# Edge attention in a graph transformer: exponentials kept in PSUM, gathers of 128 rows, and a first stage with its transfers rearranged

## The chip, the cores and the metric

The kernel runs on one core of a Trainium2 chip. A core has five engines with instruction queues of their own: TensorE (PE, matrix products and transposes), the vector engine (DVE), ScalarE (ACT), GpSimd (POOL) and SyncE (SP), which here only issues transfers. Engines wait for one another by semaphores. Transfers run on 16 DMA engines that the core's queues share. Data lie in SBUF, matrix products land in PSUM, and tables between stages are in DRAM. The metric is the device time of one execution in microseconds (us), given as a median of several runs; lower is better.

## The reference

The input is a graph with 3125 nodes of 256 features and 100,000 edges, sorted by their target node, with 64 features on each edge. Two layers follow one another. Layer 0 adds an edge attention and a mixer to the node features, then a mixture of experts; layer 1 adds a graph convolution, a linear-attention mixer and a feed-forward part on selected rows. The changed lines belong to layer 0. Its edge attention is:

```python
Q = (h @ Wq).reshape(n, H, HD)          # h = layernorm(x), H = 8 heads, HD = 32
K = (h @ Wk).reshape(n, H, HD)
V = (h @ Wv).reshape(n, H, HD)
score = jnp.einsum('ehd,ehd->eh', Q[dst], K[src]) / np.sqrt(HD)
score = score + jax.nn.relu(efeat @ W1 + b1) @ W2 + b2
m = jax.ops.segment_max(score, dst, num_segments=n)
ex = jnp.exp(score - m[dst])
denom = jax.ops.segment_sum(ex, dst, num_segments=n)
alpha = ex / denom[dst]
out = jax.ops.segment_sum(alpha[:, :, None] * V[src], dst, num_segments=n)
return out.reshape(n, D) @ Wo + bo
```

`x = x + attention(layernorm(x)) + mixer(layernorm(x))` follows, where the mixer ends with a bias `b2`; so the two constant rows `bo` and `b2` can be added to `x` early.

## The kernel before, in words

**Node rows.** The 3125 nodes are held as 125 partitions by 25 tiles. `X` is a view of them over three big SBUF tiles, `KV0` to `KV2`, which later serve as buffers of gathered rows.

**First stage (up to about 350 us).** Weights and small rows are loaded; a row that is copied to all partitions comes by `load_row` (L176). `b2` and `bo` are summed (L313), and their column form `bcol` too (L314). A loop of five steps normalises the rows (L316 to L325); GpSimd adds the normalised row and `b2` to `X` (L323, L324). A Python generator, `tables()`, builds index tables from the sorted edges: it loads the source and target nodes, the target of the next edge (`nxt`, L338 to L342), and near its end runs four indirect loads on GpSimd (`we`, L495), whose results TensorE transposes and the vector engine copies (L502). The projection loop over 25 tiles (L546 to L566) takes three steps of that generator per tile, projects keys and values into a DRAM table `kv_tab`, and queries, split in three bfloat16 parts, into `q_tab`; the split subtracts on GpSimd (L565). Then come the zero fills of the DRAM tables `o_tab`, `og_tab`, `y_tab` (L575, issued by ScalarE) and `moe_in` (L577, L579, issued by GpSimd), though the scheduler that orders each engine's instructions may place them earlier, as they depend on nothing but their zero tile. A loop over the 25 tiles computes keys and values of the mixer (L611 to L625), with vector engine, ScalarE and TensorE in turn, and a last one adds the mixer to `X` (L675 to L687). `move` (L162) is the helper that stores and loads tables in pieces.

**Edge stage (about 396 to 1710 us).** The edges are cut into 40 groups of 20 tiles of 125 edges; the 20 tiles are four runs of five. One pass of the loop (L875 to L988) handles a group. Here an order is written out by hand for TensorE (`pe`), and the vector engine's order is that of the program with the scheduler's moves. The steps, with the lines that the change or the prediction touches:

- SP loads the edge features two groups ahead (`load_features`, L763), and query rows and target indices of the group.
- GpSimd gathers one row of `kv_tab` (key and value, 512 numbers) for each edge: 20 indirect loads of 125 rows (L901), into one of ten `KV` buffers per run. Ten buffers of five tiles let 50 gathers run ahead.
- TensorE copies each edge's query from the window of target nodes (L911); the vector engine multiplies it with the gathered key, reading the query in PSUM (L914), and sums over the head (L924). In between, TensorE and ScalarE compute the next group's hidden edge features (L783, L785).
- The maximum over the group is found (L929 to L942) and subtracted (L944).
- ScalarE takes the exponential of each of the four runs and writes it next to the value columns of the `KV` buffer (L948); the vector engine multiplies the values with it (L950); TensorE sums the products by target node with a one-hot matrix (L953), for two runs in turn.
- The sums are laid into a window, divided and stored (L715, L719, L971 onward). The next group's one-hot matrix (L697) may be written only when L953 has read the present one.

Lines that say how the gathered rows, the exponentials and the sums are joined:

```python
ex = kvs[r][:, :, 2 * D:2 * D + H]
nc.scalar.activation(ex, sc[:, r * KB:(r + 1) * KB, :], AF.Exp)
v = kvs[r][:, :, D:2 * D].rearrange("p g (h d) -> p g h d", d=HD)
nc.vector.tensor_tensor(v, v, ex[:, :, :, None].to_broadcast([P, KB, H, HD]), ALU.mult)
```

Later stages (about 1710 us to the end) build the adjacency matrix (L1295), run the experts and layer 1; of the change only `load_row` reaches them.

Of the kernel before, what the change touches and what calls it, by code (L numbers as in the profile page):

```python
# [9 lines left out]
F32 = mybir.dt.float32  # L10
BF16 = mybir.dt.bfloat16
I32 = mybir.dt.int32
# [65 lines left out]
def kernel(ctx: ExitStack, tc: tile.TileContext, a, out):  # L78
# [38 lines left out]
    def row(t, shape):  # L117
        return t[:, None, :].to_broadcast(shape)
# [54 lines left out]
        nc.sync.dma_start(t, src.rearrange("(c p) n -> p c n", p=128))  # L173
        return t

    def load_row(pool, src, name, parts=P):  # L176
        n = 1
        for s in src.shape:
            n *= s
        t = pool.tile([parts, n], F32, name=name)  # L180
        nc.sync.dma_start(t, rows_of(src, parts))
        return t

    def rstd(o, var, scale=1.0):

# [86 lines left out]
    lgx = keep.tile([P, T, NE], F32, name="lgx")  # L272

    x1 = ctx.enter_context(tc.tile_pool(name="x1", bufs=1))
    KV = [x1.tile([P, KB, 2 * D + H + 1], F32, name=f"KV{i}") for i in range(3)]
    X = Rows(KV)
    with_edges = ctx.enter_context(ExitStack())
    edges = with_edges.enter_context(tc.tile_pool(name="edges", bufs=1))
    srcs = edges.tile([P, NG * GT], I32, name="srcs")
    dl = edges.tile([P, NG * GT], F32, name="dl")  # L280
    first = edges.tile([128, NG * NR], F32, name="first")
    runpos = edges.tile([128, NG], F32, name="runpos")
# [13 lines left out]
    with tc.tile_pool(name="a1", bufs=1) as a1, tc.tile_pool(name="a2", bufs=2) as a2, \  # L296
# [13 lines left out]
        bcol = a1.tile([128, 2, 2], F32, name="bcol")  # L310
        for i, n in enumerate(("L0_mix_b2", "L0_gnn_bo")):
            nc.scalar.dma_start(bcol[:, i, :], a[n].rearrange("(c p) -> p c", p=128))
        nc.vector.tensor_add(b2, b2, bo)  # L313
        nc.vector.tensor_add(bcol[:, 0, :], bcol[:, 0, :], bcol[:, 1, :])  # L314
        std = a1.tile([P, T], F32, name="std")
        for g in range(0, T, 5):  # L316
            xn = a2.tile([P, 5, D], F32, name="xn")
            mv, rs = layernorm(a2, xn, X[:, g:g + 5, :], "ln0")
            nc.scalar.activation(mean0[:, g:g + 5], mv[:, :, 0], AF.Copy)
            nc.vector.reciprocal(std[:, g:g + 5], rs)  # L320
            nc.scalar.activation(std[:, g:g + 5], std[:, g:g + 5], AF.Copy, bias=1.0)
            for i in range(5):
                nc.gpsimd.tensor_add(X[:, g + i, :], X[:, g + i, :], xn[:, i, :])  # L323
                nc.gpsimd.tensor_add(X[:, g + i, :], X[:, g + i, :], b2)  # L324
            transpose_tokens(pa, xT[:, :, g:g + 5, :], xn)  # L325
        def tables():

            with tc.tile_pool(name="c0", bufs=1) as c0:
# [6 lines left out]
                with tc.tile_pool(name="c1", bufs=1) as c1:  # L335
                    nxt = c1.tile([RP, 2 * RUN], I32, name="nxt")
                    nc.vector.memset(nxt, N)
                    yield  # L338
                    after = a["dst"][1:]
                    n = (RP - 1) * 2 * RUN  # L340
                    nc.scalar.dma_start(nxt[:RP - 1, :], after[:n].rearrange(flat, p=RP - 1))
                    nc.scalar.dma_start(nxt[RP - 1:, :2 * RUN - 1], after[n:].rearrange(flat, p=1))  # L342
                    nc.vector.tensor_tensor(nxt, nxt, dr, ALU.is_lt)
                    yield
# [201 lines left out]
        for t in range(T):  # L546
            for _ in range(3):
                next(edge_tables, None)
            ps = pa.tile([128, 512], F32, name="mm", bufs=2)
            mm(ps[:P], [(xT[:, k, t, :], wkv[:, k, :]) for k in range(2)])  # L550
            kvt = a2.tile([P, 2 * D], F32, name="kvt", bufs=3)
            evac(kvt, ps[:P])
            move(nc.sync, kv_rows[:, t, :], kvt)

            ps = pa.tile([128, 512], F32, name="mm", bufs=2)
            mm(ps[:P, :DG], [(xT[:, k, t, :], wq[:, k, :]) for k in range(2)])

            nc.vector.scalar_tensor_tensor(lgx[:, t, :], ps[:P, D:DG], std[:, t:t + 1], gb, op0=ALU.mult, op1=ALU.add)
            q = a2.tile([P, D], F32, name="q", bufs=3)
            nc.scalar.activation(q, ps[:P, :D], AF.Copy, scale=1.0 / math.sqrt(HD))  # L560
            q3 = a2.tile([P, 3, D], BF16, name="q3", bufs=3)
            for i in range(3):
                nc.scalar.activation(q3[:, i, :], q, AF.Copy)
                if i < 2:
                    nc.gpsimd.tensor_sub(q, q, q3[:, i, :])  # L565
            move(nc.sync, q_rows[:, t, :], q3.rearrange("p i d -> p (i d)"))  # L566
        for _ in edge_tables:
            pass


        zero = a3.tile([128, D + 2], F32, name="zero")
        nc.gpsimd.memset(zero[:, :D + 1], 0.0)
        nc.gpsimd.memset(zero[:, D + 1:], SKIP)
        for tab, w in ((o_tab, D), (og_tab, NE + 1), (y_tab, D)):
            move(nc.scalar, tab[:N].rearrange("(p t) c -> p t c", t=T), row(zero[:P, :w], [P, T, w]))  # L575
        whole = NE * CAP // 128 * 128
        nc.gpsimd.dma_start(moe_in[:whole].rearrange("(p k) d -> p k d", p=128),  # L577
                            row(zero, [128, whole // 128, D + 2]))
# [143 lines left out]
    with tc.tile_pool(name="l1", bufs=1) as l1, tc.tile_pool(name="l2", bufs=2) as l2, \  # L722
# [12 lines left out]
        KV = KV + [l1.tile([P, KB, 2 * D + H + 1], F32, name=f"KV{i}") for i in range(3, NKV)]  # L735
# [24 lines left out]
        efTs, hids, scts, biases = {}, {}, {}, {}  # L760

        def load_features(g):
            nc.sync.dma_start(EF[g % 2][:, :FJ, :].rearrange("p j f -> p (j f)"), efv[:, g, :])  # L763

        def turn_features(g):
            efT = efTs[g] = l2.tile([128, PF, F2], F32, name="efT")
# [108 lines left out]
        for g in range(NG):  # L875
# [17 lines left out]
            for z in range(2):  # L893
                pair = []
                for r in range(2 * z, 2 * z + 2):
                    kv = KV[nkv % NKV]
                    nkv += 1
                    pair.append(kv)
                    for i in range(KB):
                        e = g * GT + r * KB + i  # L900
                        nc.gpsimd.indirect_dma_start(out=kv[:, i, :2 * D], out_offset=None, in_=kv_tab,  # L901
                                                     in_offset=indirect(srcs[:, e:e + 1]))
# [39 lines left out]
            nc.vector.tensor_max(top, old, tps[:, :H])  # L942
            tops.append(top)
            nc.vector.tensor_sub(sc, sc, row(top[:P], [P, GT, H]))  # L944
            for z in range(2):
                for r in range(2 * z, 2 * z + 2):
                    ex = kvs[r][:, :, 2 * D:2 * D + H]
                    nc.scalar.activation(ex, sc[:, r * KB:(r + 1) * KB, :], AF.Exp)  # L948
                    v = kvs[r][:, :, D:2 * D].rearrange("p g (h d) -> p g h d", d=HD)
                    nc.vector.tensor_tensor(v, v, ex[:, :, :, None].to_broadcast([P, KB, H, HD]), ALU.mult)  # L950
                for i in range(KB):
                    for r in range(2 * z, 2 * z + 2):
                        pe(nc.tensor.matmul(seg[r * W:(r + 1) * W, :], oh[:, r * KB + i, :], kvs[r][:, i, D:],  # L953
                                            start=i == 0, stop=i == KB - 1))
# [968 lines left out]
```

## Time and profile before

| | us |
|---|---|
| median of three runs | 2893.51 (2891.22 to 2893.81) |
| profiled execution | 2897.13 |
| its span, first instruction to last | 2895.3 |
| busy in the span: TensorE / vector engine / GpSimd / ScalarE | 2240.8 / 1875.0 / 1364.6 / 934.7 |
| mean granted TensorE clock | 0.897 |
| edge stage, first product L914 | from 396.1 |
| last multiplication L950 begins | 1700.2 |
| bytes moved by DMA | 340 MB, 118 GB/s in the mean |

The profiled execution is one run taken with the hardware profiler. A line of its page that names a group reads: source line, engine, operation, what is written and read, how often; then busy time, mean duration of one in ns; then the idle time of that engine just before these instructions, and what ended most of it ("releaser"). A line of waits reads: engine, what waited and its line, for which engine and line; total us, times, longest. A line of the timeline reads: start, duration, engine, line, operation, what is written and read, how many in a row; in brackets the idle time before and its releaser. A line of one group's durations gives the shortest, the median and the longest in ns, then the start of the first and of the last.

### The profile page before, as it was taken

The numbers are of one execution on the slowest core, as the hardware profiler recorded it, in microseconds if no ns is written. First come the engines' busy times: TensorE is split into PE (matmuls) and PEld (weight loads), VectorE is DVE, ScalarE is ACT, GpSimd is POOL, SyncE is SP. The second block draws the span as 40 slices with busy tenths as digits, with TensorE's granted clock in tenths as the row PEclk, the third lists the DMA queues.
The fourth block names the chain that finished last, engine by engine and source line by source line (L and its number), as shares of the span: only waits on it lengthen the run. The fifth ranks groups of instructions, "written<-read, shape, count | busy, mean of one in ns | idle before, by whom it ended". The sixth has DMA issues, their size and how long they took to land. (4 is left out here: it accounts for less than half of the span.)

```text
span 2895.3 us, 40359 instructions
## 1 busy us (share of the span) xinstructions
PE 2240.8 (77%) x14013; PEld 1404.5 (49%) x14013; DVE 1875.0 (65%) x4137; ACT 934.7 (32%) x1838; POOL 1364.6 (47%) x1172
## 2 busy tenths in 40 slices
PE   2588777777777777787777744799689999978894
PEld 1244434444444444444444323465457775756673
DVE  4748337777777777777777658343478844846446
ACT  0243133333333333333333304212163323243331
POOL 3444368888888887788888712211100002221110
PEclk9788869999998999989999866899899999999997
DMA  7740488888888888888888842233200002000001
GB/s 187 159 126 17 109 192 191 183 193 190 188 193 190 187 195 187 190 188 189 191 194 191 184 111 85 79 98 105 55 2 5 5 1 70 2 1 1 1 19 48
DMA packets 272347, 340.23 MB, mean 118 GB/s; under 512 B 156170, under 2 KB 203437, under 8 KB 271534
## 3 DMA queue, kind: packets, MB, share of 16 engines
q0 software_dynamic: 185600, 219.53, 33.4%
q1 hardware_dynamic: 72794, 101.95, 13.5%
q10 hardware_dynamic: 13732, 16.01, 2.2%
q8 instruction: 114, 1.87, 0.3%
q14 instruction: 107, 0.88, 0.1%
HBM read 294.80 MB, written 43.25 MB: 117 GB/s over the span
## 5 line engine op out<-in xcount | busy, mean ns | idle before, releaser
L901 POOL DMA_INDIRECT KV<-kv_tab,srcs x800 | 1077.4, 1347 | 330.2 <-issue 148.9
L914 DVE TENSOR_TENSOR KV<-KV,qe 125x512 f32<-125x512 f32 (+1 forms) x480 | 266.3, 595 | 154.9 <-PE qe L911 142.9
L953 PE MATMUL seg<-KV,oh 125*32 125x265 f32 x1600 | 267.6, 525 | 126.3 <-DVE KV L950 115.6
L785 ACT ACTIVATE hid<-hidden,b1e 128x910 f32<-128x910 f32 (+1 forms) x240 | 249.5, 1039 | 304.0 <-PE hidden L783 304.0
L911 PE MATMUL qe<-q,ohT 64*125 64x256 bf16 x2400 | 220.2, 280 | 98.5 <-DVE KV L914 95.5
L911 PEld LDWEIGHTS <-ohT 64*125 64x125 bf16 x2400 | 159.7, 134 | 218.3 <-issue 210.8
L783 PE MATMUL hidden<-efT,w1e 64*128 64x455 f32 (+1 forms) x960 | 240.3, 574 | 16.1 <-ACT hid L785 14.7
L953 PEld LDWEIGHTS seg<-KV,oh 125*32 125x32 f32 x1600 | 133.0, 143 | 244.7 <-DVE KV L950 160.8
L924 DVE TENSOR_REDUCE sc<-KV 125x40 f32<-125x1280 f32 x160 | 229.9, 1478 | 0.0
L950 DVE TENSOR_TENSOR KV<-KV 125x1280 f32<-125x1280 f32 x160 | 227.9, 1487 | 1.5 <-ACT KV L948 1.4
L1493 PE MATMUL sum<-adj,f 125*128 125x400 bf16 (+1 forms) x1050 | 197.2, 328 | 0.0
L1295 PE MATMUL build<-oc,op 128*125 128x200 bf16 x1176 | 144.0, 262 | 55.9 <-ACT xn L214 41.4
L192 DVE TENSOR_TENSOR op<-values,ends_of 128x756 bf16<-128x756 bf16 x196 | 108.3, 553 | 93.4 <-PE build L1295 91.5
L1295 PEld LDWEIGHTS <-op 128*125 128x125 bf16 x1176 | 125.8, 144 | 82.3 <-ACT xn L214 41.5
L1493 PEld LDWEIGHTS <-f 125*128 125x128 bf16 x1200 | 115.7, 98 | 102.9 <-issue 31.2
L192 DVE TENSOR_TENSOR oc<-values,ends_of 128x1200 bf16<-128x1200 bf16 x196 | 152.3, 777 | 0.0
L1562 POOL DMA_DIRECT2D ln_cols<-in_L_mix_ln_g_dram x1 | 0.8, 787 | 316.3 <-DVEq L1513 316.3
L1298 ACT ACTIVATE adj<-build 125x400 bf16<-125x400 f32 x171 | 86.0, 504 | 186.0 <-PE build L1295 186.0
L715 ACT ACTIVATE u<-seg 128x265 f32<-128x265 f32 x40 | 15.7, 393 | 332.3 <-PE seg L953 332.3
L1619 PE MATMUL mm<-bt,fw 128*128 128x250 f32 (+1 forms) x416 | 100.8, 405 | 26.4 <-DVE bt L110 23.3
L265 PE MATMUL mm<-bt,w 128*128 128x489 f32 x256 | 110.5, 582 | 5.1 <-ACT bt L112 3.3
L265 PE MATMUL mm<-w,hT 128*128 128x256 f32 (+1 forms) x512 | 112.6, 379 | 0.0
(462 smaller groups left out, 3910.4 us busy)
## 6 DMA issues: line engine op xcount, KB each, us to landing
EF<-in_edge_attr_dram SPq DMA_DIRECT2D x40, 625.0 KB
w<-in_L_ffn_w_dram SPq DMA_DIRECT2D x16, 1024.0 KB
KV<-kv_tab,srcs POOLq DMA_INDIRECT x800
q<-q_tab SPq DMA_DIRECT2D x160, 48.0 KB
dlb<-dl_tab SPq DMA_DIRECT2D x160, 39.1 KB
kv_tab<-kvt SPq DMA_DIRECT2D x25, 224.0 KB
o_tab<-ow SPq DMA_DIRECT2D x40, 128.0 KB
q_tab<-q SPq DMA_DIRECT2D x25, 168.0 KB
```

Of the source, the lines that this page charges most:

```text
L192: nc.vector.tensor_tensor(dst.rearrange("p n (m o) -> p n m o", o=2), values.rearrange("p (u m o) -> p u m o", u=1, o=2).to_broadcast([dst ...
L265: nc.tensor.matmul(o, l, r, start=i == 0, stop=i == len(pairs) - 1)
L783: pe(nc.tensor.matmul(ps[:, s, :n * F2], w1e[f, c * 128:(c + 1) * 128], efTs[g][f, p0:p0 + n, :], start=True, stop=True))
L785: nc.scalar.activation(hids[g][:, c, p0:p0 + n, :].rearrange("h p (f s) -> h s p f", s=2), ps[:, :, :n * F2].rearrange("h s (p f) -> h s p ...
L901: nc.gpsimd.indirect_dma_start(out=kv[:, i, :2 * D], out_offset=None, in_=kv_tab, in_offset=indirect(srcs[:, e:e + 1]))
L911: pe(nc.tensor.matmul(ps[:, i, :], ohT[w, z, (i0 + i) * P:(i0 + i + 1) * P], q3[w, z, k, :], start=k == 0, stop=k == 2))
L914: nc.vector.tensor_mul(kv[:, i0:i0 + nt, :D], kv[:, i0:i0 + nt, :D], ps[:, :nt, :])
L924: nc.vector.tensor_reduce(sc[:, r0:r0 + KB, :], kv[:, :, :D].rearrange("p g (h d) -> p g h d", d=HD), AX.X, ALU.add)
L950: nc.vector.tensor_tensor(v, v, ex[:, :, :, None].to_broadcast([P, KB, H, HD]), ALU.mult)
L953: pe(nc.tensor.matmul(seg[r * W:(r + 1) * W, :], oh[:, r * KB + i, :], kvs[r][:, i, D:], start=i == 0, stop=i == KB - 1))
L1295: pe(nc.tensor.matmul(ps[:, j // CT, :], op[:, j, :P], oc[:, j, :], start=j % CT == 0, stop=j % CT == CT - 1))
L1493: pe(nc.tensor.matmul(sps[c][:, :n], f3[:, t, i, c * 128:(c + 1) * 128], adj[:, t, :n], start=t == 0 and i == 0, stop=t == T - 1 and i == 2))
```

## The change

Four edits come together.

1. **Exponentials.** Per group two exponentials of two runs each replace four of one run. They are written to a PSUM tile that shares the buffer name `score` with the tile of the edge scores. The vector engine's multiplication reads them there, and ScalarE copies them run by run from PSUM to the columns of the `KV` buffer that L953 reads.
2. **Gathers.** The `KV` buffers and the index table have 128 partitions instead of 125; each gather moves 128 rows. The three additional indices are set to zero, and what they bring is not read.
3. **Edge features.** A group's load of 100 partitions is issued as two, of 96 and of 4.
4. **First stage.** `load_row` loads 128 partitions everywhere. The sums with `bo` stand behind the layernorm loop, and `b2` is added to `X` in a loop of its own. The load of `nxt`, 79 partitions, is issued as 64 and 15. The zero tile is tied behind the last query subtraction of the projections, so that the zero fills can't start before; three of the four tables are now filled by SP's queue instead of ScalarE's.

```diff
-    def load_row(pool, src, name, parts=P):
+    def load_row(pool, src, name):
...
-        t = pool.tile([parts, n], F32, name=name)
-        nc.sync.dma_start(t, rows_of(src, parts))
-        return t
+        t = pool.tile([128, n], F32, name=name)
+        nc.sync.dma_start(t, rows_of(src, 128))
+        return t[:P]
...
-    srcs = edges.tile([P, NG * GT], I32, name="srcs")
+    all_srcs = edges.tile([128, NG * GT], I32, name="srcs")
+    nc.gpsimd.memset(all_srcs[96:], 0)
+    srcs = all_srcs[:P]
...
-        nc.vector.tensor_add(b2, b2, bo)
-        nc.vector.tensor_add(bcol[:, 0, :], bcol[:, 0, :], bcol[:, 1, :])
...
-                nc.gpsimd.tensor_add(X[:, g + i, :], X[:, g + i, :], b2)
             transpose_tokens(pa, xT[:, :, g:g + 5, :], xn)
+        nc.vector.tensor_add(bcol[:, 0, :], bcol[:, 0, :], bcol[:, 1, :])
+        nc.vector.tensor_add(b2, b2, bo)
+        for t in range(T):
+            nc.gpsimd.tensor_add(X[:, t, :], X[:, t, :], b2)
...
+                    for p0, p1 in ((0, (RP - 1) // 16 * 16), ((RP - 1) // 16 * 16, RP - 1)):
+                        nc.scalar.dma_start(nxt[p0:p1, :],
+                                            after[p0 * 2 * RUN:p1 * 2 * RUN].rearrange(flat, p=p1 - p0))
                     n = (RP - 1) * 2 * RUN
-                    nc.scalar.dma_start(nxt[:RP - 1, :], after[:n].rearrange(flat, p=RP - 1))
...
-                    nc.gpsimd.tensor_sub(q, q, q3[:, i, :])
+                    rest = nc.gpsimd.tensor_sub(q, q, q3[:, i, :])
...
-        nc.gpsimd.memset(zero[:, :D + 1], 0.0)
-        nc.gpsimd.memset(zero[:, D + 1:], SKIP)
+
+        for x in (nc.gpsimd.memset(zero[:, :D + 1], 0.0), nc.gpsimd.memset(zero[:, D + 1:], SKIP)):
+            tc.add_manual_dep(x.ins, rest.ins.name, NOSYNC, reason="zeros behind the projections")
         for tab, w in ((o_tab, D), (og_tab, NE + 1), (y_tab, D)):
-            move(nc.scalar, tab[:N].rearrange("(p t) c -> p t c", t=T), row(zero[:P, :w], [P, T, w]))
+            move(nc.sync, tab[:N].rearrange("(p t) c -> p t c", t=T), row(zero[:P, :w], [P, T, w]))
...
-            nc.sync.dma_start(EF[g % 2][:, :FJ, :].rearrange("p j f -> p (j f)"), efv[:, g, :])
+            for r in (slice(0, PF // 16 * 16), slice(PF // 16 * 16, PF)):
+                nc.sync.dma_start(EF[g % 2][r, :FJ, :].rearrange("p j f -> p (j f)"), efv[r, g, :])
...
-                        nc.gpsimd.indirect_dma_start(out=kv[:, i, :2 * D], out_offset=None, in_=kv_tab,
-                                                     in_offset=indirect(srcs[:, e:e + 1]))
+                        nc.gpsimd.indirect_dma_start(out=whole[:, i, :2 * D], out_offset=None, in_=kv_tab,
+                                                     in_offset=indirect(all_srcs[:, e:e + 1]))
...
+            exps = pl.tile([128, 3, P], F32, name="score")[:P].rearrange("p a b -> p (a b)")
+            exps = exps[:, :GT * H].rearrange("p (j h) -> p j h", h=H)
             for z in range(2):
+                part = slice(2 * z * KB, 2 * (z + 1) * KB)
+                nc.scalar.activation(exps[:, part, :], sc[:, part, :], AF.Exp)
                 for r in range(2 * z, 2 * z + 2):
-                    ex = kvs[r][:, :, 2 * D:2 * D + H]
-                    nc.scalar.activation(ex, sc[:, r * KB:(r + 1) * KB, :], AF.Exp)
+                    ex = exps[:, r * KB:(r + 1) * KB, :]
                     v = kvs[r][:, :, D:2 * D].rearrange("p g (h d) -> p g h d", d=HD)
                     nc.vector.tensor_tensor(v, v, ex[:, :, :, None].to_broadcast([P, KB, H, HD]), ALU.mult)
+                    nc.scalar.activation(kvs[r][:, :, 2 * D:2 * D + H], ex, AF.Copy)
```

The rest of the diff gives the ten `KV` buffers 128 partitions (`WHOLE`), with `KV` as their first 125.

More of the change, by code (lines that the diff above doesn't have):

```diff
@@ L274 @@
     x1 = ctx.enter_context(tc.tile_pool(name="x1", bufs=1))
-    KV = [x1.tile([P, KB, 2 * D + H + 1], F32, name=f"KV{i}") for i in range(3)]
+    WHOLE = [x1.tile([128, KB, 2 * D + H + 1], F32, name=f"KV{i}") for i in range(3)]
+    KV = [t[:P] for t in WHOLE]
     X = Rows(KV)
@@ L734 @@
             nc.sync.dma_start(b2e[W * c:W * c + H, :], a["L0_gnn_b2"].rearrange("(h o) -> h o", o=1))
-        KV = KV + [l1.tile([P, KB, 2 * D + H + 1], F32, name=f"KV{i}") for i in range(3, NKV)]
+        WHOLE = WHOLE + [l1.tile([128, KB, 2 * D + H + 1], F32, name=f"KV{i}") for i in range(3, NKV)]
+        KV = [t[:P] for t in WHOLE]
         for t in KV:
@@ L895 @@
                 for r in range(2 * z, 2 * z + 2):
-                    kv = KV[nkv % NKV]
+                    kv, whole = KV[nkv % NKV], WHOLE[nkv % NKV]
                     nkv += 1
```

## The prediction

> **What bounds the kernel now.** I read the page's costliest groups first, then the vector engine's waits inside the edge stage (400 to 1710 us), then one group of that stage in order of time, then the stretches of the first stage. The edge stage is 45% of the span and takes two of the parts changed. Its groups on the page:
>
> ```profile
> L901 POOL DMA_INDIRECT KV<-kv_tab,srcs x800 | 1077.4, 1347 | 330.2 <-issue 148.9
> L914 DVE TENSOR_TENSOR KV<-KV,qe 125x512 f32<-125x512 f32 (+1 forms) x480 | 266.3, 595 | 154.9 <-PE qe L911 142.9
> L953 PE MATMUL seg<-KV,oh 125*32 125x265 f32 x1600 | 267.6, 525 | 126.3 <-DVE KV L950 115.6
> L924 DVE TENSOR_REDUCE sc<-KV 125x40 f32<-125x1280 f32 x160 | 229.9, 1478 | 0.0
> L950 DVE TENSOR_TENSOR KV<-KV 125x1280 f32<-125x1280 f32 x160 | 227.9, 1487 | 1.5 <-ACT KV L948 1.4
> ```
>
> GpSimd's gathers (L901) are the largest sum, 1077 us, so GpSimd looks like the bound. The vector engine's waits say otherwise:
>
> ```profile
> DVE KV L914 <- PE qe L911: 139.2, 196, 1.4
> DVE oh L697 <- PE seg L953: 114.8, 38, 4.1
> ...
> DVE KV L914 <- issue: 7.4, 1, 7.4
> DVE KV L914 <- DMA KV<-kv_tab,srcs: 4.6, 6, 1.1
> ```
>
> It waits 139 us for TensorE's query products and 115 us (38 times, 3.0 each) for the segment sums, and 12 us in all for gathers. L950 starts at 416.3 first and 1700.2 last: 39 groups in 1284 less 5, 32.8 us each. GpSimd needs 20 x (1.347 + about 0.3 between two gathers) = 32.9 for the same, so it falls slowly behind: counted in the trace, 39 gathers are issued ahead at the first group and 18 near the end, out of 50 that ten buffers allow. The lead nearly lasts. What sets the pace is the chain vector engine, TensorE, ScalarE within a group. Its softmax part, from the timeline of one group:
>
> ```profile
> 934.12 0.61 ACT L948 ACTIVATE KV<-sc 125x40 f32<-125x40 f32 x4 [0.57 <-DVE sc L944]
> ...
> 934.39 5.70 DVE L950 TENSOR_TENSOR KV<-KV 125x1280 f32<-125x1280 f32 x4
> ...
> 934.99 1.96 POOL L901 DMA_INDIRECT KV<-kv_tab,srcs  x1 [0.30 <-DMA KV<-kv_tab,srcs]
> ...
> 937.25 2.51 POOL L901 DMA_INDIRECT KV<-kv_tab,srcs  x1 [0.31 <-DMA KV<-kv_tab,srcs]
> 937.34 5.31 PE L953 MATMUL seg<-KV,oh 125*32 125x265 f32 x32 [0.31 <-DVE KV L950]
> 940.07 1.18 POOL L901 DMA_INDIRECT KV<-kv_tab,srcs  x1 [0.30 <-DMA KV<-kv_tab,srcs]
> ...
> 943.36 0.83 DVE L697 TENSOR_TENSOR oh<-dl,iota 125x640 f32<-125x640 f32 x1 [3.27 <-PE seg L953]
> ```
>
> The four exponentials run ahead of the four multiplications, which stand back to back (5.70). Then the vector engine waits 3.27 until the sums that follow the last of them are done. Beside L950 a gather takes 1.96 and 2.51 instead of 1.2; L950 itself never takes over 1494 ns.
>
> **Part 1, exponentials by way of PSUM.** Two exponentials of 125x80 replace four of 125x40, and four ScalarE copies of 125x40 bring the result into the columns that the segment sums read. All lie in one PSUM tile. In the built program each copy waits for its run's multiplication, the next multiplication for that copy, the second exponential for the second copy. So the phase is one file: exp, mul, copy, mul, copy, exp, mul, copy, mul, copy. Durations: the multiplication 1.487 (L950; the product L914 reads PSUM and takes 0.68 for 512 columns, L950 1.487 for 1280: the same 1.05 ns per column, so PSUM as an input costs nothing); exp of 125x40 0.226, of 1x8 0.19, hence 125x80 about 0.26; a copy out of PSUM of 125x64 0.22 and of 125x96 0.25 (L808), hence 125x40 about 0.20; each hand-over ScalarE to vector engine and back about 0.03. The phase becomes 4 x 1.487 + (0.20+0.06) + (0.20+0.26+0.09) + (0.20+0.06) = 7.02 against 5.70: +1.32. The first exponential is 0.03 longer. The last run's sums wait for its copy: +0.23. Given back: the first pair's sums now have 3.5 instead of 3.0 us before the last pair's, so less is queued: 0.25. Sum +1.33 per group, x 40 = **+53 us**. Ends: group by group the tail from last multiplication to last sum is 2.48 to 4.09, mean 3.01; if all fall to 2.48, 1.58 - 0.53 = +1.05 (+42); if TensorE, less busy, takes all at the slow end, 1.58 + 1.08 = +2.66 (+106). I take the middle as the tail keeps its nine matmuls (two records each) of some 0.31: in the timeline 19 run from 937.34 to 943.32.
>
> Here a rule of the Trainium skill is weighed ("PSUM — Partial Sum Buffer", section on bank collisions): two engines on one bank and partition quadrant must be kept apart, two readers too. The row is L948's four in 0.61 with 1.4 us of waiting for ScalarE in the whole stage: in SBUF both read freely. By that row the copies would run beside the next multiplication and only 0.03 + 0.23 be added, +10 us over 40 groups. By the rule +53. The waits in the built program follow the rule, so I take it.
>
> **Part 2, gathers of 128 rows; L950 with one SBUF input.** Another rule speaks for the change ("SBUF — State Buffer", "Who interferes with whom"): a vector instruction with two SBUF inputs contends with a GpSimd instruction that reads SBUF, one with a single SBUF input does not. The two stretched gathers above agree: 0.76 + 1.31 = 2.1 us per group. Rows for the size:
>
> ```profile
> L1442 POOL DMA_INDIRECT y_tab<-yr,who x32: 974/982/1071, 1856.5 to 2075.8; - x32
> L1385 POOL DMA_INDIRECT moe_in<-xn,pi x25: 1191/1194/1695, 1784.8 to 1823.6; - x25
> ```
>
> 128 rows are issued in 0.98, 125 rows in 1.19. GpSimd's need falls to 20 x 1.28 + 0.9 (L192, L697 still stretch some) = 26.5 per group. If GpSimd set the pace, 20 x 0.22 + 2.1 = 6.5 x 40 = 260 us could go; by the waits only the 12 us for gathers can: **-12** (0 to -13). 2.4% more rows raise the DMA share from 0.83 to 0.85 in a longer period: nothing, covered by the lead of the gathers; without cover 2.4% of 27 us busy, 0.6 per group.
>
> **Part 3, features.** 96 + 4 rows instead of 100: SP issues one more DMA of 0.33 per group, loaded two groups ahead: 0; SP has no wait on the path there.
>
> **Part 4, first stage.** The zero fills (10.2 MB) move from the first 130 us to behind the projections' last query subtraction (L565), the large one still on GpSimd's queue, the others from ScalarE's to SP's; the bias sums move behind the layernorm; one more GpSimd loop adds b2 (same 25 additions, moved).
>
> ```profile
> DVE bcol L314 <- DMA bcol<-in_L_gnn_bo_dram: 17.5, 1, 17.5
> DVE b L313 <- DMA bo<-in_L_gnn_bo_dram: 11.9, 1, 11.9
> ...
> 100.00:150.00 50.00, 23.48 (x48) 11.23 (x48) 31.98 (x38) 12.34 (x29) 12.08 (x16) 0.69 0.83 177
> 150.00:210.00 60.00, 53.05 (x149) 27.74 (x150) 24.36 (x52) 30.32 (x76) 25.70 (x37) 0.93 0.48 142
> 210.00:275.00 65.00, 56.14 (x199) 30.87 (x198) 59.84 (x108) 21.53 (x46) 34.10 (x27) 0.92 0.08 28
> ```
>
> (columns of the last three: length, busy of TensorE, its loads, vector engine, ScalarE, GpSimd, granted clock, DMA share, GB/s.) L565 runs from 90.8 to 204.2; from 163 on it takes 3.11 per tile, so 25 tiles are worth 78 and 35 are lost to waits while the DMA engines are full. With GpSimd's wait of 16.1 for the bias, at most 35 + 16 = 51 us can go. But at 210 to 275 the vector engine is the bound (59.84 of 65), and that stage's work does not shrink. It also gets work: the table steps that were spread over the projections stand in it, and they wait for four indirect loads on GpSimd's queue (L495), of which the second stands behind the 3.87 MB zero fill. That fill took 31 us in the first stage (2.88 to 33.88); now it shares the engines with 6.25 MB more from SP, and at the 177 to 240 GB/s seen, 10 MB take 42 to 57. With the projections' end near 152 (204 - 51), the second load lands near 195 to 205 and the vector engine stands until then, with the key and value products (L621, L623) queued behind it. Then 60 us of that stage (as now, 213.9 to 273.9) end at 255 to 265 instead of 274: -9 to -19. Some tiles of it can run before the stall: **-18**. Ends: -50 if the second load slips past the fill, +8 if the fills also hold SP's stores of the tables.
>
> **Part 5, rows of 128 partitions in load_row.** One such load (mb) stands 6.9 us on the chain at 2395.5; halved or so: **-2** (0 to -5).
>
> **Sum:** +53 - 12 - 18 - 2 = +21. The profiled execution took 2897.13 (span 2895.3 and 1.8 around it), 3.6 above the median; differences carry over, so 2893.5 + 21 = **2914 us**, and a profile near 2918.
>
> **The rivals.** *First stage wins (faster).* The serial file costs its low end, +42, and the zero fills don't hold the vector engine: -50 - 12 - 4. Net -24: 2869. It turns at one point, whether the second indirect load waits for the 3.87 MB: below zero once the first stage gives more than 39 at +53, or more than 28 at +42. For it: 51 us of waits; against: one queue. *TensorE slows.* Every tail at 4.09: +106 - 12 - 18 - 2 = +74: 2968. For it: TensorE idles some 0.5 us more between pairs, and its clock row varies from 0.69 to 0.93 by stretch; against: in the mean the tail is 3.01. *The file isn't one.* Copies beside multiplications: +10 - 12 - 18 - 2 = -22: 2871; against it the waits in the built program. *It evens out* at 2893: first stage -40 with +53 - 12.
>
> **How the numbers follow.** Likeliest 0.60 (its own range 2898 to 2935), first stage wins 0.18, file isn't one 0.05, evens out 0.07, TensorE slows 0.10. Two per mille, 5.8 us, is about what a measurement can tell from no change. Faster 0.18 + 0.05 = 0.23; same 0.07; slower 0.60 + 0.10 = 0.70. Range: half of the faster cases are cut below 2870, and half of the slow end above 2962.
>
> **What would show it.** Right: the multiplication (L964) stays at 1.49 with gaps of 0.26, 0.55, 0.26 in a group and 7.0 us in all; gathers at 0.98 and none of 2 us beside L964; a period near 34.1; waits of L914 for gathers gone; the vector engine idle for some 35 us for the second indirect load; first product (L924) near 378 instead of 396. Wrong: multiplications back to back, a period under 33.5 or over 35, or a kv stage that ends before 245.

## The result, and the profile after

The changed kernel takes 2932.95 us (median of four, 2928.93 to 2939.47), the kernel before beside it 2893.49: ratio 1.0139, interval 1.0121 to 1.0156. It is slower by 39.5 us; 21 were forecast. Two later comparisons gave 1.0149 (1.0131 to 1.0166) and 1.0139 (1.0108 to 1.0170).

The two profiled executions lie nearer: spans of 2927.1 and 2895.3, 31.8 apart. The execution profiled before was 3.6 above its median, the one after (2928.93) 4.0 below its own; 31.8 + 3.6 + 4.0 = 39.4. By stretches of the span:

| us | before | after | difference |
|---|---|---|---|
| start to first query product | 396.1 | 378.0 | -18.1 |
| first product to end of the last value multiplication | 1305.6 | 1356.9 | +51.3 |
| from there to the end | 1193.6 | 1192.2 | -1.4 |

The groups on the page after, in the form of those shown of before (L924 is now the product, L964 the multiplication, L965 the copy, L968 the sums, L911 the gathers):

```profile
L911 POOL DMA_INDIRECT KV<-kv_tab,srcs x800 | 760.0, 950 | 653.6 <-PE seg L968 398.3
L968 PE MATMUL seg<-KV,oh 125*32 125x265 f32 x1600 | 315.5, 565 | 147.0 <-ACT KV L965 147.0
L924 DVE TENSOR_TENSOR KV<-KV,qe 125x512 f32<-125x512 f32 (+1 forms) x480 | 265.9, 595 | 148.6 <-PE qe L921 148.6
...
L964 DVE TENSOR_TENSOR KV<-KV,score 125x1280 f32<-125x1280 f32 x160 | 238.1, 1488 | 45.8 <-ACT score L960 23.9
...
L965 ACT ACTIVATE KV<-score 125x40 f32<-125x40 f32 x160 | 33.1, 207 | 243.7 <-DVE KV L964 243.7
```

GpSimd's gathers are busy 760 us instead of 1077, and GpSimd now waits 398 us ahead of them for the sums that free its buffers: it is far ahead. The multiplication takes 1488 ns as before, but has 45.8 us of idle time where it had 1.5. The vector engine's waits from 400 to 1750 us:

```profile
DVE KV L924 <- PE qe L921: 142.2, 194, 1.4
DVE oh L705 <- PE seg L968: 126.5, 38, 3.5
...
DVE KV L964 <- ACT score L960: 22.6, 43, 0.5
DVE KV L964 <- ACT KV L965: 21.9, 80, 0.3
```

The two waits that the prediction counted as waits for gathers (7.4 and 4.6) are gone; two for ScalarE have come, and the one for the sums has grown from 114.8 to 126.5. One group in order of time:

```profile
1011.53 0.24 ACT L960 ACTIVATE score<-sc 125x80 f32<-125x80 f32 x1 [0.69 <-DVE f L975]
...
1011.80 1.49 DVE L964 TENSOR_TENSOR KV<-KV,score 125x1280 f32<-125x1280 f32 x1
1013.32 0.21 ACT L965 ACTIVATE KV<-score 125x40 f32<-125x40 f32 x1 [1.43 <-DVE KV L964]
1013.56 1.49 DVE L964 TENSOR_TENSOR KV<-KV,score 125x1280 f32<-125x1280 f32 x1 [0.27 <-ACT KV L965]
...
1015.08 0.21 ACT L965 ACTIVATE KV<-score 125x40 f32<-125x40 f32 x1 [1.55 <-DVE KV L964]
1015.32 0.24 ACT L960 ACTIVATE score<-sc 125x80 f32<-125x80 f32 x1
...
1015.34 6.13 PE L968 MATMUL seg<-KV,oh 125*32 125x265 f32 x34 [0.67 <-ACT KV L965]
1015.59 1.49 DVE L964 TENSOR_TENSOR KV<-KV,score 125x1280 f32<-125x1280 f32 x1 [0.55 <-ACT score L960]
...
1018.88 0.21 ACT L965 ACTIVATE KV<-score 125x40 f32<-125x40 f32 x1 [1.55 <-DVE KV L964]
...
1022.18 0.82 DVE L705 TENSOR_TENSOR oh<-dl,iota 125x640 f32<-125x640 f32 x1 [3.33 <-PE seg L968]
```

Read the starts downward: in these lines ScalarE and the vector engine never work at the same time. Each copy begins when its multiplication ends, each multiplication when the copy ends. The gaps are 0.27, 0.55 and 0.27, and the phase, from the start of the first multiplication to the end of the fourth, is 7.04 us.

### The profile page after: what moved, and what is told of

Same layout as the page of the kernel before. It is cut to its first block, busy times and chain, and to the rows that moved or that the text cites. A ratio compares the mean times of both kernels' runs of the same rounds, so it can differ in the third digit from the quotient of the medians.

```text
span 2927.1 us, 40409 instructions
## 1 busy us (share of the span) xinstructions
PE 2283.7 (78%) x14013; PEld 1386.7 (47%) x14013; DVE 1876.5 (64%) x4137; ACT 964.6 (33%) x1918; POOL 1052.8 (36%) x1173
## 5 line engine op out<-in xcount | busy, mean ns | idle before, releaser
L911 POOL DMA_INDIRECT KV<-kv_tab,srcs x800 | 760.0, 950 | 653.6 <-PE seg L968 398.3
L968 PE MATMUL seg<-KV,oh 125*32 125x265 f32 x1600 | 315.5, 565 | 147.0 <-ACT KV L965 147.0
L924 DVE TENSOR_TENSOR KV<-KV,qe 125x512 f32<-125x512 f32 (+1 forms) x480 | 265.9, 595 | 148.6 <-PE qe L921 148.6
L968 PEld LDWEIGHTS seg<-KV,oh 125*32 125x32 f32 x1600 | 121.8, 149 | 324.5 <-ACT KV L965 186.6
L964 DVE TENSOR_TENSOR KV<-KV,score 125x1280 f32<-125x1280 f32 x160 | 238.1, 1488 | 45.8 <-ACT score L960 23.9
L793 PE MATMUL hidden<-efT,w1e 64*128 64x455 f32 (+1 forms) x960 | 237.2, 566 | 13.9 <-ACT hid L795 12.3
L705 DVE TENSOR_TENSOR oh<-dl,iota 125x640 f32<-125x640 f32 x40 | 33.0, 824 | 126.5 <-PE seg L968 126.5
L965 ACT ACTIVATE KV<-score 125x40 f32<-125x40 f32 x160 | 33.1, 207 | 243.7 <-DVE KV L964 243.7
```

The lines of the kernel that those rows point to most:

```text
L793: pe(nc.tensor.matmul(ps[:, s, :n * F2], w1e[f, c * 128:(c + 1) * 128], efTs[g][f, p0:p0 + n, :], start=True, stop=True))
L911: nc.gpsimd.indirect_dma_start(out=whole[:, i, :2 * D], out_offset=None, in_=kv_tab, in_offset=indirect(all_srcs[:, e:e + 1]))
L924: nc.vector.tensor_mul(kv[:, i0:i0 + nt, :D], kv[:, i0:i0 + nt, :D], ps[:, :nt, :])
```

## The experiments

Phases are read from the profile of each run and averaged over the groups: the four multiplications with their gaps, the tail from the last multiplication to the last sum, the loop from the first product to the last multiplication. Theory: the copies and the multiplications of one PSUM tile form one serial file (each waits for the one before), and that is the loss; the gathers gain what was late, no more. First rival: freeing GpSimd from the vector engine's second SBUF input pays. Second rival: TensorE's clock is the loss.

**The change again, after_again and after_third.** Nothing is edited.

> The changed kernel once more, beside the single parts. If its spread lies in the clock granted to TensorE and not in the order of the work, the period of a group stays at 34.1 us and the four multiplications at 7.04 us, and the time falls between 2929 and 2940 us. If the profiled execution was only luckily early in the first stage, the first product comes later than 378 us here.

Measured: 2929.66 and, on another chip, 2934.28, with first products at 377.0 and 380.3, loops of 1356.3 and 1356.5, the multiplications at 7.04 both times. The loop repeats to 0.6 us; what varies is the rest. The first product was not early by chance in the first profile. The expectation of the second one belongs to a later experiment:

> The changed kernel once more, because four kernels with gathers of 128 rows took 3540 to 3630 us on one chip, where the kernel before took 2910, with TensorE standing for 5 to 10 us at a time inside groups. If that belongs to those kernels, the changed kernel takes 2929 to 2940 us here with a period of 34.1 us. If it belongs to a chip together with 128-row gathers, the changed kernel takes 3550 us or more wherever the other two kernels of this call do, and all three are fast elsewhere.

**The exponentials alone.** The kernel before, with only this edit:

```diff
+            exps = pl.tile([128, 3, P], F32, name="score")[:P].rearrange("p a b -> p (a b)")
+            exps = exps[:, :GT * H].rearrange("p (j h) -> p j h", h=H)
             for z in range(2):
+                part = slice(2 * z * KB, 2 * (z + 1) * KB)
+                nc.scalar.activation(exps[:, part, :], sc[:, part, :], AF.Exp)
                 for r in range(2 * z, 2 * z + 2):
-                    ex = kvs[r][:, :, 2 * D:2 * D + H]
-                    nc.scalar.activation(ex, sc[:, r * KB:(r + 1) * KB, :], AF.Exp)
+                    ex = exps[:, r * KB:(r + 1) * KB, :]
...
+                    nc.scalar.activation(kvs[r][:, :, 2 * D:2 * D + H], ex, AF.Copy)
```

> Only the exponentials by way of PSUM, on the kernel before. Theory (one serial file per group): multiplications 7.04 us per group instead of 5.70, tail 0.3 longer, so +1.7 x 40 = +66 us, less up to 13 us of late gathers because the period of about 34.1 us now leaves GpSimd enough time for 20 gathers of 125 rows: about 2893 + 53 = 2946 us, first product still near 396 us, gathers none over 1.9 us beside the multiplication. Rival (freeing GpSimd from the vector engine's second SBUF input pays): at or under 2893 us.

Measured: 2943.64, ratio 1.0197 (1.0177 to 1.0217), +55 against 2888.57 on that chip. The multiplications take 7.04, the loop 1356.6, the same as in the whole change. The vector engine's waits show the same two for ScalarE, and none for a gather:

```profile
DVE oh L697 <- PE seg L957: 125.2, 38, 3.4
...
DVE KV L953 <- ACT score L949: 23.8, 44, 1.3
DVE KV L953 <- ACT KV L954: 21.8, 80, 0.3
```

So this edit alone makes the loss in the loop, and neither wider gathers nor split feature loads move the loop once it is in. It also ends the late gathers with 125 rows: the period of 34.1 leaves GpSimd time enough. That no gather beside the multiplication would take over 1.9 us did not hold (27 do, 98 before), but nothing waits for them. The first rival falls: GpSimd is relieved of the second SBUF input here, and the kernel is slower. Against this kernel the whole change (2929.66 on the same chip) is 14.0 us faster, and its first product comes 13.9 us earlier: that is what all its other parts are worth once the exponentials are in.

**All but the exponentials.** The changed kernel with the exponentials and multiplications (L948, L950) of before.

> The changed kernel with the exponentials of the kernel before. Theory: period back to about 32.5 us with multiplications back to back (5.70), first product at 378 us, no product waits for gathers, as 128 rows take 0.95 us even where some are stretched beside the multiplication: 2893 - 18 - 13 - 2 = about 2861 us. Rival (the gathers need the relief of the PSUM operand): the lead of the gathers falls again and late ones stretch groups, over 2875 us.

Measured: 2866.55, ratio 0.9920 (0.9896 to 0.9945), -22 where -32 were expected. The loop is right (1292.1, that is 13.5 under the 1305.6 of before, and no product waits for a gather), with stretched gathers left beside the multiplication (mean 1.03 us instead of 0.95). The difference lies outside: the first product comes at 381.9, and the exponentials-alone kernel, whose first stage is that of before, has it at 390.9 on this chip, not 396.1.

**The first stage alone.** The kernel before with the zero fills, the bias sums, the split of `nxt` and the 128-row loads of the change.

> Only the first stage's changes and the 128-row loads, on the kernel before. Theory: first product near 378 us, -18, and -2 in the last layer; the gathers stay at 125 rows and fall behind as before, so late gathers cost 13 us again: about 2873 us. Rival (the earlier start gives the gathers no lead or costs it): above 2880 us, with products waiting longer for gathers than 12 us.

Measured: 2885.08, ratio 0.9990 (0.9978 to 1.0002): not told from no change, -3.5 where -20 were expected. First product at 384.9 against 390.9; loop 1305.8, as before; from the last multiplication to the end 1195.8, nothing gained there. So of what looked like 18 us in the first stage, 6 on this chip belong to these edits; another 3 to 8 (381.9 with all but the exponentials, 377.0 with all) come with the gathers of 128 rows. The trace shows where: the stretch from the mixer's last key and value sum to the first product is 120.7 to 122.3 us in three profiles with the old gathers and 113.9 to 118.2 in five with the new ones (on chips without the trouble described below, fills as in the change), and in it the first loads of query rows and target indices land in some 7.2 us in the change and in some 13.2 here. (Those kernels also have the split feature loads, which were not tried apart.) The rest is variation between executions.

**The gathers alone, on the kernel before.** The buffers and the index table are as in the change.

```diff
-                        nc.gpsimd.indirect_dma_start(out=kv[:, i, :2 * D], out_offset=None, in_=kv_tab,
-                                                     in_offset=indirect(srcs[:, e:e + 1]))
+                        nc.gpsimd.indirect_dma_start(out=whole[:, i, :2 * D], out_offset=None, in_=kv_tab,
+                                                     in_offset=indirect(all_srcs[:, e:e + 1]))
```

> Only the gathers of 128 rows, on the kernel before. Theory: about 1.03 us in the mean (some stretched beside the multiplication), no late group, loop near 1292 us instead of 1305.6; and the edge stage's first loads land a few us sooner, as the first gathers leave the DMA engines more room: 2889 - 13 - 5 = about 2871 us. Rival (the lead was never short): 2886 us or more.

Measured: 3563.87, ratio 1.2257, on a chip where the kernel before took 2910.53. Neither expectation foresaw this; the last experiment of this section returns to it. Undisturbed, the wide gathers are worth 18.5 us, read from all but the exponentials against the first stage alone on one chip (2866.55 and 2885.08, the split feature loads included); 13.7 of it are in the loop.

**Exponentials in two PSUM tiles by turns.** The changed kernel, and each run's exponential in another tile than its neighbour's:

```diff
-            exps = pl.tile([128, 3, P], F32, name="score")[:P].rearrange("p a b -> p (a b)")
...
-                nc.scalar.activation(exps[:, part, :], sc[:, part, :], AF.Exp)
...
                 for r in range(2 * z, 2 * z + 2):
-                    ex = exps[:, r * KB:(r + 1) * KB, :]
+                    exps = pl.tile([P, 2, D], F32, name="qe", bufs=2)
+                    ex = exps.rearrange("p a d -> p (a d)")[:, :KB * H].rearrange("p (j h) -> p j h", h=H)
+                    nc.scalar.activation(ex, sc[:, r * KB:(r + 1) * KB, :], AF.Exp)
```

> The changed kernel, but with an exponential for each run again, written by turns into the two PSUM tiles of the query products; multiplication and copy as in the change. Theory (two readers of one PSUM tile are kept apart, and that alone makes the serial file): a copy now shares its tile only with its own run's multiplication, so the four multiplications stand back to back, 5.7 to 5.8 us instead of 7.04, and only the copy of 0.2 ahead of the last sums remains: period about 32.7 us, some 2870 us. Rival (the length comes from reading PSUM in the multiplication, or from ScalarE's hand-overs as such): 6.7 us or more, over 2915 us.

On the chip of gathers alone it took 3624.33 too, but its multiplications stood back to back (5.68). Again, on a chip without that trouble:

> The changed kernel, the exponential of each run written by turns into the two PSUM tiles of the query products, multiplication and copy as in the change. In the disturbed run its four multiplications stood back to back (5.68 us) and the tail was 3.27. Theory (readers of one PSUM tile kept apart make the serial file): undisturbed the period is 32.7 us and the time 2870 us. Rival (the shorter phase is given back in the tail or the next group): over 2900 us.

Measured: 2883.10, ratio 0.9943 (0.9922 to 0.9964), with a period of 32.83. The period is as expected, the time 13 us over the 2870 expected; the excess lies outside the loop. From the timeline of one group:

```profile
1022.74 0.33 ACT L960 ACTIVATE qe<-sc 125x40 f32<-125x40 f32 x2 [0.70 <-DVE f L973]
...
1022.98 5.68 DVE L962 TENSOR_TENSOR KV<-KV,qe 125x1280 f32<-125x1280 f32 x4
...
1024.50 0.21 ACT L963 ACTIVATE KV<-qe 125x40 f32<-125x40 f32 x1 [1.30 <-DVE KV L962]
1024.74 0.21 ACT L960 ACTIVATE qe<-sc 125x40 f32<-125x40 f32 x1
...
1025.90 0.21 ACT L963 ACTIVATE KV<-qe 125x40 f32<-125x40 f32 x1 [0.95 <-DVE KV L962]
```

The copies at 1024.50 and 1025.90 now lie within the 5.68 of the multiplications. Four copies and a PSUM operand are still there, and the exponentials are four instead of two; what is gone is the sharing of one tile. The loop is 1305.6: 51 us under the change, and 14 over the 1291.1 of the kernel with the zero fills last (below), which has no copies. So of the 65 us that the exponentials cost a loop without late gathers, 51 go with the shared tile; the other 14 lie in the tail, 3.42 us instead of 3.01, where the last run's copy comes ahead of the sums. On the phase the theory holds.

**Exponentials twice, no copies.** One of 125x160 into PSUM for the multiplications, four of 125x40 straight into the buffers' columns.

> The changed kernel, but without copies: one exponential of 125x160 into PSUM for the multiplications, and four of 125x40 straight into the columns of the KV buffers for the sums. Theory: multiplications back to back (5.70), the first some 0.1 later, no copy ahead of the sums: period 32.5 to 32.6 us, about 2865 us, with gathers at 0.95 us beside the multiplication. Rival (TensorE's clock or the tail is the cost, not the file): over 2890 us.

> The kernel with the zero fills behind the last indirect load, with one exponential of 125x160 into PSUM for the four multiplications and four of 125x40 straight into the columns of the KV buffers, and no copies. Theory (the gathers have lead enough, so freeing GpSimd from the multiplication's second SBUF input is worth nothing): multiplications back to back at 5.70, each group's first some 0.1 us later, loop 1291 + 4 = 1295 us, about 2850 us, gathers 0.95 instead of 1.03 us. Rival (the relief of GpSimd pays): loop under 1288 us, under 2843 us.

Both ran on chips with the trouble described below: 3616.82, and with the fills of the next experiment 3615.81 (beside 2910.53 and 2984.10). Their times say nothing on the question. In both the multiplications read the one PSUM tile, which ScalarE only writes once per group, and stand back to back at 5.68: reading PSUM does not by itself lengthen them. The first comes 0.13 us later than with exponentials in SBUF; whether the relief of GpSimd pays by itself stays open in the time. Since no product waits for a gather in all but the exponentials, I see no place in which it could.

**The zero fills later.** The changed kernel with the exponentials of before, and the zero tile tied behind the last of the four indirect loads:

```diff
-            tc.add_manual_dep(x.ins, rest.ins.name, NOSYNC, reason="zeros behind the projections")
+            tc.add_manual_dep(x.ins, lasts[0].ins.name, NOSYNC, reason="zeros behind the projections")
```

> The changed kernel with the exponentials of the kernel before, and the zero fills tied behind the last indirect load of the table steps instead of the last query subtraction. Theory (the second indirect load stands behind the 3.87 MB fill and the vector engine with it, 13.1 us): each of the four loads takes about 5 us, key and value sums of the mixer end some 13 to 20 us before 262, first product at 360 to 368 us, about 2850 us. Rival (the fill now falls on the mixer's end and the first gathers): first product not before 376 us, 2860 us or more.

> The changed kernel with the exponentials of the kernel before and the zero fills behind the last indirect load of the table steps. In the disturbed run its first product came at 380.1 against 397.9 and 405.1 us of two kernels beside it. Theory: undisturbed the first product comes at 360 to 368 us and the time is about 2850 us, 15 under the same kernel with the fills behind the query subtraction. Rival: the fills are paid for at the first gathers, first product at 376 us or later, 2860 us or more.

The first run fell on the troubled chip (3545.60); its first product at 380.1 came 18 us ahead of its neighbour's 397.9 there. The second: 2845.85, ratio 0.9837 (0.9806 to 0.9868), first product at 357.3, loop 1291.1. GpSimd's order in the change shows the second load (L502) behind the fill:

```profile
162.05 1.66 POOL L585 DMA_DIRECT2D moe_in<-zero  x1 [0.30 <-POOL zero L580]
167.08 1.02 POOL L502 DMA_INDIRECT we<-ec_tab,found_i  x1 [3.37 <-PE prep L507]
168.09 0.59 POOL L587 DMA_DIRECT2D moe_in<-zero  x1
...
194.47 1.24 POOL L502 DMA_INDIRECT we<-ec_tab,found_i  x1 [0.16 <-issue]
...
207.89 0.89 POOL L502 DMA_INDIRECT we<-ec_tab,found_i  x1 [10.89 <-PE prep L507]
```

and with the fills last:

```profile
158.36 1.05 POOL L503 DMA_INDIRECT we<-ec_tab,found_i  x1 [3.10 <-DVE found_i L500]
...
166.90 0.95 POOL L503 DMA_INDIRECT we<-ec_tab,found_i  x1 [2.20 <-PE prep L508]
...
173.23 0.96 POOL L503 DMA_INDIRECT we<-ec_tab,found_i  x1 [0.75 <-PE prep L508]
...
178.31 0.89 POOL L503 DMA_INDIRECT we<-ec_tab,found_i  x1 [0.86 <-PE prep L508]
179.21 0.37 POOL L581 MEMSET zero<- 128x257 f32 x2
...
180.74 1.73 POOL L586 DMA_DIRECT2D moe_in<-zero  x1
```

In the change the second load, issued at 167.08 behind the 3.87 MB fill, lands at 189.78, 22.7 us later and 1.1 after the fill (188.66); with the fills last it takes 3.65. In two more profiles of that order it lands 0.6 and 1.0 us after the fill. Whether the order on GpSimd's queue alone holds it back is not shown: the third load, issued at 194.47 with no fill left ahead of it on that queue but with SP's fills under way, takes 11.5. The mixer's key and value sums end at 238.2 instead of 262.6. The fills then run from 180 to 235, while few other transfers are under way. This kernel is faster than the kernel before and than all but the exponentials.

**The trouble on two chips.** On one chip four kernels took 3546 to 3624 us where the kernel before took 2910.53, on a second one 3615.81 where it took 2984.10. All of them have gathers of 128 rows. Two of them (two tiles by turns, and the fills last) took 2883.10 and 2845.85 elsewhere, and no kernel with such gathers met the trouble on the other chips used here. From the timeline of the gathers-alone kernel (the releaser "remote" is an event that the profile couldn't assign to an instruction):

```profile
995.23 1.89 PE L787 MATMUL hidden<-efT,w1e 64*128 64x455 f32 x4 [0.53 <-issue]
...
1005.98 1.28 DVE L918 TENSOR_TENSOR KV<-KV,qe 125x512 f32<-125x512 f32 x2 [12.78 <-remote]
1006.08 1.08 ACT L789 ACTIVATE hid<-hidden,b1e 128x910 f32<-128x910 f32 x1 [10.90 <-remote]
1006.72 0.37 PE L915 MATMUL qe<-q,ohT 64*125 64x256 bf16 x1 [9.61 <-DVE KV L918]
```

TensorE's matrix products are recorded until about 997, and the vector engine and ScalarE, which wait for products, both go on only at 1006. The vector engine's waits of this kind from 420 to 1600 us are

```profile
DVE KV L918 <- remote: 368.2, 50, 18.7
```

and the granted clock is at half for 55% of that time, against 16% in the kernel before (profiled on another chip). All 368 us lie while a burst of 20 gathers is issued and lands (taken as 3.9 us after the last issue), which is 61% of the time. In the kernel before there are no bursts, as GpSimd never stops for long. That is no proof that the bursts are the cause: each starts at its group's sums and so falls on the same steps of every group, and the same bursts are harmless on the other chips. They were not taken away as a test. What in these chips makes TensorE stand is open, and so is whether the whole change would stand there too: it met three times chips where it didn't.

## Why the prediction was right

| us | forecast | found |
|---|---|---|
| exponentials, in the loop | +53 | +65 |
| late gathers, in the loop | -12 | -14 |
| up to the first product | -18 | -18 |
| after the loop | -2 | -1 |
| place of the two profiled executions among their runs | 0 | +7.6 |
| sum | +21 | +39.5 |

The direction and the main mechanism were right; the sum fell short by 18.5 us. Of that, 10 are in the loop, where the tail was sized too small, and 7.6 are the difference between profiles and medians. The first stage's number fits in part by luck.

**What bounds the kernel.** Right: the chain within a group. The exponentials-alone kernel shows it from one side (+55 us with GpSimd relieved) and all but the exponentials from the other (260 us of gather time at stake by the prediction's estimate, 13.5 gained in the loop).

**Part 1, the serial file.** Right in mechanism and nearly in every term: phase 7.04 (7.02 forecast), exponential 0.24 (0.26), copy 0.21 (0.20), gaps 0.27, 0.55, 0.27 (0.26, 0.55, 0.26), period 34.1. The weighing of the Trainium skill's rule on bank collisions ("PSUM — Partial Sum Buffer") against the row of before came out for the rule: +10 by the row, +53 by the rule; two tiles by turns cost 14 and one tile 65. What is shown is that the program as built keeps the two readers apart, by semaphores; no run lets them collide.

The mis-sized term is what happens to the tail, from the last multiplication to the last sum: +0.23 for the copy less 0.25 "given back", so nothing in all. It is 3.31 us, against 3.01 before. Some was given back, but the tail also follows the clock that TensorE is granted, which the forecast took as unchanged. Three tails, two of before and one of the change (columns as in the prediction's stretches, the clock third from the end):

```profile
1037.70:1040.18 2.48, 2.48 (x29) 1.69 (x23) 0.00 (x0) 0.00 (x0) 2.18 (x2) 1.00 0.57 144
1668.95:1672.97 4.02, 4.02 (x31) 2.74 (x27) 0.00 (x1) 0.00 (x0) 3.41 (x3) 0.60 0.90 219
```

```profile
1018.84:1022.14 3.30, 3.30 (x26) 1.47 (x22) 0.00 (x1) 0.21 (x1) 2.38 (x4) 0.77 0.70 202
```

Length times clock is 2.41 to 2.48 in each of the 40 tails of before, mean 2.44, and 2.54 to 2.55 in those of the change. So the copy, less what came back, adds 0.10 us at full clock. But 13 of the 40 tails of before had full clock, and none of the change's; the mean fell from 0.835 to 0.77. At the clocks as granted, the work makes 0.13 of the 0.30 and the lower clock 0.17. Why the clock is lower in every tail was not tested. Instead of +1.33 a group it was 1.34 (phase) + 0.07 (first exponential, forecast 0.03) + 0.30 (tail) = +1.71, in 40 groups +68, not +53; the loops with and without the edit differ by 64 to 66.

**Part 2, gathers.** Late gathers cost 12 by the waits; they gave 13.5 in the loop of all but the exponentials. Most of it is one group near the end, 41.85 us from its first product to the next group's, against some 32.5 for the others; no group of the change is so long. The sum took the gain for one of the wide gathers; the slower file would have brought it too, as the exponentials-alone loop, 1356.6, shows. The Trainium skill's rule on shared ports ("SBUF — State Buffer", "Who interferes with whom") agrees: from 420 to 1600 us 105 of 707 gathers took over 1.7 us before, none of 690 after; but GpSimd's ease was worth nothing where GpSimd didn't set the pace.

**Part 3.** Nothing, as forecast: the loop is the same within 0.3 us with parts 2 and 3 (the change) and without them (exponentials alone).

**Part 4, the first stage.** -18 forecast, -18.1 in the profile, and the stall was where it was put: `found_i` (L499) waits for the second indirect load, which lands at 189.78 (195 to 205 forecast). But the wait is 13.1 us, not 35, and the number is right in part by luck: the mixer's key and value sums end at 262.6 (255 to 265 forecast) instead of 274.3, which is -12, and the other 6 come later, where the first loads of the edge stage land sooner beside the wide gathers, an effect that part 2 put at nothing. It also rests on one pair of executions. First stages like that of before reached the first product at 396.1 and 390.9, those of the change with wide gathers at 377.0 to 381.9; on one chip the medians give 14.0 for all parts but the exponentials, and the first stage alone gave 3.5.

The rival "first stage wins" turned on that one load, and the kernel with the fills last shows what it held: its first product comes 39 us earlier than 396.1, and without the change's exponentials it is 52 us under the kernel before. With them, +65, it would by this sum still be slower; that was not run.

**Part 5.** -2 forecast, -1.5 to +2.1 over three profiles of the change: not told from nothing. The wait for `mb` on the chain (6.9) is replaced by one for `ln1g` of 4.8: the wait moved to another row's load.

**The rivals.** "TensorE slows" is refuted as the main cause: the granted clock from 420 to 1600 us is 0.90 in place of 0.92, with two tiles it is 0.91 and the 51 us are gone. It has a share of some 7 us (0.17 in 40 tails), where it was given +53 for every tail at its slowest. "The file isn't one" is refuted by the gaps. "It evens out" needed 40 us from the first stage and got 14 to 18.

## What to carry to other kernels

Ask of a PSUM tile that two engines read in turn how many pieces of work share it: the readers follow one another, and an engine that was free to run ahead is put into the file of the other. Give each piece a tile of its own, or don't go by way of PSUM. Relief for an engine is worth what the waits for it say, not what its busy time says. A fill that depends on nothing should stand behind the small transfers that others wait for, not ahead of them. When a step that ends in matrix products is moved, check the clock granted there before and after: a tail can grow without more work.

## What the runs showed that I had not expected

Three more rows per gather changed the transfers as a whole, not only their issue. The software queue on the two pages, before and after (packets, MB, share of the 16 engines):

```profile
q0 software_dynamic: 185600, 219.53, 33.4%
```

```profile
q0 software_dynamic: 70400, 223.56, 26.5%
```

Other transfers are in these sums too. From 420 to 1600 us, where the queue carries gathers only, one of 125 rows made 224 packets, 132 of them of 8 bytes; one of 128 rows makes 80, none of 8 bytes. It moves more bytes, and yet at about the same rate (189 and 187 GB/s) the DMA engines' share falls from 0.83 to 0.66. I had expected it to rise by 2.4%.

Kernels with gathers of 128 rows took 21 to 24% longer than the kernel before on two chips, through stands of TensorE (above). One chip's comparison, on which a kernel looks 2% better, would have told nothing of that.
